# A fused FFN, attention, FFN block on one core: FFN mix read from PSUM, mask merged into the bias, square on ScalarE, 16-bit projections, PSUM banks shared in pairs

## The chip, the core and the metric

The kernel runs on one NeuronCore of a Trainium2 chip. The metric is device time in microseconds (us). The engines are named as the profile names them: PE (TensorE, matmuls), PEld (its weight loads), DVE (VectorE), ACT (ScalarE), POOL (GpSimd) and SP (SyncE, which here issues nearly all DMAs).

## The reference, cut to what matters

Eight sequences of 1024 positions and 256 features go through three residual steps.

```python
x = x + 0.5 * ffn(layernorm(x))
x = x + attn(layernorm(x))
x = x + 0.5 * ffn(layernorm(x))

def ffn(x, W_r, W_k, W_v, mu_r, mu_k):           # x_prev: x shifted by one position, 0 at the start
    xr = mu_r * x + (1 - mu_r) * x_prev
    xk = mu_k * x + (1 - mu_k) * x_prev
    r = sigmoid(xr @ W_r.T)
    return r * (square(relu(xk @ W_k.T)) @ W_v.T)

def attn(x, ...):                                # 16 heads of 16 features
    q, k, v = split(x @ qkv_w.T + qkv_b)
    # 40 offsets: 0..32, 48, 64, 96, 128, 192, 256, 384
    lg[i] = (q . shift(k, o_i)) / 4 * (1 + q @ scale_embed[i]) + pos_bias[i]   # -1e30 where pos < o_i
    out = sum_i softmax(lg)[i] * shift(v, o_i)
    return ((out * if_gain) * sigmoid(x @ gate_w.T + gate_b)) @ out_w.T + out_b
```

## The kernel before, in words

The 8192 rows are cut into 32 chunks of 256 positions and 64 tiles of 128. Five generators hold the work: `stage_f1` (first FFN, by chunk), `stage_p` (the four projections, by chunk), `stage_qk` (scores of queries with local and far keys, by half a sequence), `stage_att` (the rest of the attention, by tile) and `stage_f2` (second FFN, by chunk). A list of steps at the end of the kernel interleaves them, with the stages lagging each other by fixed amounts. Each step gets a priority, and the Tile layer then orders the instructions of each engine by a simulated timeline; each engine executes its own order strictly, waiting on semaphores for the others. So the order on every engine is fixed when the kernel is built.

A chunk of an FFN (`ffn`) takes its PSUM tiles from one bank per lane: tag "ps" plus the lane's letter, "a" for the first FFN and "b" for the second, "p" for the projections. In that bank follow each other the transposed normalized input `tr` (L162), the product with `wk`, that with `wr` and that with `wv` (all recorded at L134, the helper `mm`). Between them stand the copy of `tr` to SBUF with a column for the previous position (`xt`, L186, and the small POOL instructions L183, L185, L189), the difference and the two mixes on DVE (L193, L196), relu and tanh on ACT (L201, L206), the square on POOL (L207), the gating on DVE (L212) and the residual add on POOL (L213).

The projections split the input into `xh` + `xl` and the weights into `wa_hi` + `wa_lo` and add three products for each, in float32r. Each group of q and k goes to DRAM as a 16-bit pair `hl` (L263 on ACT, L264 on DVE). `scores` (in `stage_qk`) multiplies 32-query blocks against keys on 32-column tiles of PE; its results are copied by ACT at L308 (`sl` and `sf`) and written to DRAM in a skewed layout, from where each attention tile reads its logits `lg`.

In `stage_att` `gp` (L134) holds 1 + q.scale_embed before the 1 is added, and DVE multiplies it in at L405 and L410. POOL adds the bias (L419) and, in the first three tiles of a sequence, the mask (L421). After max, subtraction and exp (L423, L424, L425) the probabilities of the 33 near offsets go to DRAM and come back skewed as `pd`, the longest round trip of the tile. The far offsets are multiplied on POOL (L445, `prod`) and added on DVE (L457). PE transposes `pd` in two halves (L464), ACT copies each to `ptt` (L470), and 32 small matmuls of a 32-column tile, 16 after each half, give `pv`. DVE normalizes (L481 to L485), PE transposes `acc` (L490), DVE gates it (L491), and every second tile PE applies the output weights `wot` and DVE adds the result to x (L505).

PSUM has eight banks, used as: one for each of lanes a, b and p, one for scores (`psq`), one for `gp`, one for `pv`, one for the transposes of `pd` (`pst`), and one for the transpose of `acc` and the output product (`psy`).

Of the kernel before, what the change touches and what calls it, by code (L numbers as in the profile page):

```python
# [8 lines left out]
F32 = mybir.dt.float32  # L9
F32R = mybir.dt.float32r  # L10
F16 = mybir.dt.float16
I32 = mybir.dt.int32
AF = mybir.ActivationFunctionType
ALU = mybir.AluOpType
# [25 lines left out]
F2A = 28  # L40
TRACE = (0, 3.6, -4.4, -8.1, -10.6)
# [8 lines left out]
def macaron(ctx: ExitStack, tc: tile.TileContext, x, wffn, watt, wo, cols, rows, pbias, se, mask, out):  # L50
# [14 lines left out]
    bias = const.tile([128, NO * 16], F32, name="bias")  # L65
    msk = const.tile([128, 3, NO], F32, name="msk")
    wa_hi = const.tile([128, 4, 2, 256], F32R, name="wa_hi")
    wa_lo = const.tile([128, 4, 2, 256], F32R, name="wa_lo")
    seb = const.tile([128, 2, NO], F16, name="seb")
    half = const.tile([128, 4], F32, name="half")  # L70
# [18 lines left out]
    def load_ffn():  # L89
        nc.sync.dma_start(w_f, wffn.rearrange("w (c p) d -> p w c d", p=128))  # L90
        nc.vector.tensor_scalar(w_f[:, 2], w_f[:, 2], 0.25, None, ALU.mult)

    def load_att():
        with tc.tile_pool(name="setup", bufs=1) as sp:
            wst = sp.tile([128, 4, 2, 256], F32, name="wst")
            nc.sync.dma_start(wst, watt.rearrange("w (c p) d -> p w c d", p=128))
            nc.vector.tensor_scalar(wst[:, 0], wst[:, 0], 0.25, None, ALU.mult)
            nc.vector.tensor_copy(wa_hi, wst)
            nc.vector.tensor_tensor(wa_lo, wst, wa_hi.bitcast(F32), ALU.subtract)
            nc.vector.tensor_scalar(b_q, b_q, 0.25, None, ALU.mult)  # L100
            nc.vector.tensor_scalar(b_g, b_g, 0.5, None, ALU.mult)
            nc.sync.dma_start(row, rows.unsqueeze(0).to_broadcast([128, 2, 256]))
            for t in [t.bitcast(F32) for t in kb] + vw:
                nc.gpsimd.memset(t, 0.0)
# [8 lines left out]
            nc.sync.dma_start(bias, pbias.to_broadcast([128, NO * 16]))  # L113
            nc.sync.dma_start(msk, mask.rearrange("t p u -> p t u"))
            nc.sync.dma_start(wot, wo.rearrange("(c p) d -> p c d", p=128))
            for c in range(2):
                nc.vector.tensor_scalar(wot[:, c], wot[:, c], gain[:, c : c + 1], 0.5, ALU.mult, ALU.mult)
# [15 lines left out]
    def mm(o, l, r, start, stop):  # L133
        nc.tensor.matmul(o, l, r, start=start, stop=stop)  # L134
# [30 lines left out]
    def ffn(take, done, lane, singles):  # L165
# [3 lines left out]
        for c in range(NCH):  # L169
# [23 lines left out]
            nc.vector.tensor_tensor(xr, xt[:, :, 1:257], prev, ALU.subtract)  # L193
            for o, mu in ((xk, mu_k), (xr, mu_r)):
                for h in range(2):
                    nc.vector.scalar_tensor_tensor(o[:, h], xr[:, h], mu[:, h : h + 1], prev[:, h], ALU.mult, ALU.add)  # L196
# [10 lines left out]
            nc.gpsimd.tensor_tensor(xk, xk, xk, ALU.mult)  # L207
# [25 lines left out]
    def stage_p():  # L233
        for c in range(NCH):
# [10 lines left out]
            nc.vector.tensor_tensor(xl, tr, xh.bitcast(F32), ALU.subtract)  # L245
# [26 lines left out]
            for g in range(2):  # L272
                nc.scalar.activation(gt[:, g], p[:, g], AF.Tanh, bias=b_g[:, g : g + 1], scale=0.5)
# [23 lines left out]
    def stage_qk():  # L297
        def scores(o, g, q4, q, k, keys):

            p = ps.tile([128, 512], F32, name="p", tag="psq")  # L300
# [7 lines left out]
            nc.scalar.copy(o[:, :, :, g], p.rearrange("n (q h j) -> n j h q", q=4, h=2))  # L308
# [60 lines left out]
    def stage_att():  # L369
        for tt in range(B * NT):  # L370
# [27 lines left out]
            for h2 in range(2):  # L398
                gp = ps.tile([128, 64, 8], F32, name="gp")
                for g in range(2):  # L400
# [5 lines left out]
                    lg[:, 0:NL, e], gp[:, 0:NL], 1.0, lg[:, 0:NL, e], ALU.add, ALU.mult  # L406
                )
                for k0, k1 in FARG:
# [4 lines left out]
                        1.0,  # L413
# [172 lines left out]
```

## Time and profile before

| what | value |
|---|---|
| median of 3 runs | 1262.62 us (1255.21 to 1265.52) |
| the profiled execution | 1256.76 us, its span 1254.0 us |
| mean granted PE clock | 0.956 |
| busy PE, PEld | 1089.2, 885.7 us |
| busy DVE, POOL, ACT | 942.6, 766.5, 538.0 us |
| DMA | 282.88 MB, mean 226 GB/s |

The busy time of an engine is the time covered by its instructions. A matmul's interval reaches from its start to the modelled end of its pipeline, and the intervals of successive matmuls overlap, so the distance between their starts is what one of them costs. PEld, the weight loads, runs beside the matmuls. "Idle before, releaser" in a profile row is the time that the engine stood before the instruction, and who ended it. A helper's matmuls all have line L134, so they are told apart by the names of their tiles.

### The profile page before, as it was taken

How to read it: one execution, taken by the hardware profiler on the slowest of the kernel's cores; microseconds unless marked ns; L12 is line 12 of the kernel's file. 1: busy time of each engine (PE TensorE's matmuls, PEld its weight loads, DVE VectorE, ACT ScalarE, POOL GpSimd, SP SyncE). 2: the span in 40 equal slices, each digit the busy share in tenths (PEclk: the TensorE clock that was granted, in tenths of full speed). 3: DMA queues.
4: the chain of work that ended last, by engine and by line, in shares of the span. 5: the costliest groups of instructions: out<-in, count | busy, mean ns of one | idle time of the engine just before them, and what ended most of it. 6: DMA issues, size and time to landing. Idle time of an engine off the chain costs nothing.

```text
span 1254.0 us, 34712 instructions
## 1 busy us (share of the span) xinstructions
PE 1089.2 (87%) x13568; PEld 885.7 (71%) x13568; DVE 942.6 (75%) x2266; ACT 538.0 (43%) x1025; POOL 766.5 (61%) x1101
## 2 busy tenths in 40 slices
PE   2887989899799898989899989899988998888785
PEld 2676768677687677777777778786777787665664
DVE  7546768987587888879678866978858887877772
ACT  2444445344453444536345454544534444524231
POOL 7436619675575656659457564867656755657672
PEclk9999999899999999899999999999989999998988
DMA  8187888786878779787788977797787868998630
GB/s 263 32 224 222 241 242 265 229 238 194 251 226 254 230 233 274 221 252 232 193 260 257 254 201 230 228 269 227 233 243 234 269 197 254 284 280 265 202 99 24
DMA packets 256500, 282.88 MB, mean 226 GB/s; under 512 B 23440, under 2 KB 214608, under 8 KB 256336
## 3 DMA queue, kind: packets, MB, share of 16 engines
q1 hardware_dynamic: 247120, 263.36, 71.7%
q10 hardware_dynamic: 9216, 17.31, 3.8%
q8 instruction: 106, 1.74, 0.6%
q14 instruction: 58, 0.48, 0.1%
HBM read 151.67 MB, written 128.91 MB: 224 GB/s over the span
## 4 chain that ended last, share of the span: by engine, by line
PE 42%; DMA 25%; DVE 14%; SPq 6%; POOL 5%; issue 5%; ACT 4%; POOLq 0%; ACTq 0%; DVEq 0%
PE p L134 29%; DMA pd<-pd 9%; PE tra L464 4%; PE pv L134 3%; PE tra L134 3%; POOL prod L445 2%; DMA lg<-sl 2%; DMA x<-in_x_dram 2%; DMA qk<-hl 2%; DMA kb<-qk 2%; DMA sl<-sl 2%; DVE prod L457 2%; DVE xk L196 1%; PE gp L134 1%; DVE mx L423 1%
## 5 line engine op out<-in xcount | busy, mean ns | idle before, releaser
L134 PEld LDWEIGHTS <-qst 128*32 128x32 f16 (+1 forms) x5120 | 157.2, 120 | 100.1 <-issue 63.5
L134 PE MATMUL p<-kb,qst 128*32 128x128 f16 (+1 forms) x4096 | 185.1, 297 | 12.7 <-ACT sl L308 8.6
L308 ACT COPY sl<-p 128x512 f32<-128x512 f32 x224 | 130.8, 584 | 144.2 <-PE p L134 123.0
L445 POOL TENSOR_TENSOR prod<-v,lg 128x256 f32<-128x256 f32 x248 | 165.5, 687 | 10.2 <-ACT lg L425 6.1
L134 PE MATMUL p<-xk,w_f 128*128 128x256 f32 x512 | 144.9, 421 | 20.0 <-DVE xk L196 11.7
L419 POOL TENSOR_TENSOR lg<-lg,bias 128x640 f32<-128x640 f32 x64 | 113.5, 1774 | 71.8 <-DVE lg L410 66.9
L213 POOL TENSOR_TENSOR x<-x,xr 128x512 f32<-128x512 f32 x64 | 88.4, 1382 | 109.0 <-DVE xr L212 94.9
L457 DVE TENSOR_TENSOR prod<-prod 128x512 f32<-128x512 f32 (+2 forms) x120 | 126.1, 1051 | 32.1 <-POOL prod L445 31.5
L464 PE MATMUL tra<-ident,pd 128*128 128x128 f32 x512 | 97.1, 313 | 58.3 <-DMA pd<-pd 54.9
L160 ACT ACTIVATE xn<-x,nb,y 128x256 f32<-128x256 f32 x192 | 110.8, 602 | 63.0 <-DVE nb L152 55.2
L134 PE MATMUL p<-w_f,xk 128*128 128x256 f32 x512 | 132.9, 400 | 1.7 <-ACT xr L206 1.3
L134 PE MATMUL p<-w_f,xr 128*128 128x256 f32 x512 | 130.4, 396 | 3.6 <-ACT xk L201 2.8
L445 POOL TENSOR_TENSOR prod<-vn,lg 128x256 f32<-128x256 f32 x144 | 96.0, 678 | 54.3 <-ACT lg L425 35.4
L134 PE MATMUL p<-xh,wa_hi 128*128 128x256 f32 x384 | 123.2, 321 | 5.6 <-DVE hl L264 4.4
L134 PEld LDWEIGHTS p<-xk,w_f 128*128 128x128 f32 x512 | 99.3, 208 | 39.8 <-issue 10.5
L470 ACT COPY ptt<-tra 128x512 f32<-128x512 f32 x128 | 74.9, 585 | 116.1 <-PE tra L464 113.0
L464 PEld LDWEIGHTS tra<-ident,pd 128*128 128x128 f32 x512 | 71.0, 197 | 73.9 <-DMA pd<-pd 68.0
L263 ACT ACTIVATE hl<-p,col 128x256 f16<-128x256 f32 x128 | 60.6, 474 | 121.1 <-PE p L134 68.6
L134 PE MATMUL p<-xh,wa_lo 128*128 128x256 f32 x384 | 111.5, 290 | 0.0
L134 PE MATMUL p<-xl,wa_hi 128*128 128x256 f32 x384 | 111.4, 290 | 0.0
L134 PEld LDWEIGHTS p<-w_f,xr 128*128 128x128 f32 x512 | 95.3, 196 | 19.4 <-ACT xk L201 5.8
L134 PEld LDWEIGHTS p<-w_f,xk 128*128 128x128 f32 x512 | 96.0, 198 | 15.9 <-issue 2.8
(82 smaller groups left out, 2394.2 us busy)
## 6 DMA issues: line engine op xcount, KB each, us to landing
qk<-hl SPq DMA_DIRECT2D x256, 128.0 KB, 3.4
sl<-sl SPq DMA_DIRECT2D x256, 128.0 KB, 3.8
pd<-pd SPq DMA_DIRECT2D x64, 512.0 KB, 4.8
sf<-sl SPq DMA_DIRECT2D x184, 128.0 KB, 3.1
vw<-vd SPq DMA_DIRECT2D x128, 136.0 KB, 4.1
v<-vd SPq DMA_DIRECT2D x64, 272.0 KB, 4.3
lg<-sl SPq DMA_DIRECT2D x64, 264.0 KB, 4.1
pd<-lg ACTq DMA_DIRECT2D x64, 264.0 KB, 3.8
```

What stands on the lines that cost most here:

```text
L134: nc.tensor.matmul(o, l, r, start=start, stop=stop)
L160: nc.scalar.activation(xn, x2[:, i], AF.Identity, bias=nb[:, k : k + 1], scale=y[:, k : k + 1])
L196: nc.vector.scalar_tensor_tensor(o[:, h], xr[:, h], mu[:, h : h + 1], prev[:, h], ALU.mult, ALU.add)
L213: nc.gpsimd.tensor_tensor(x2, x2, xr, ALU.add)
L263: nc.scalar.activation(hl[:, 0], p[:, g], AF.Identity, bias=bb[:, g : g + 1])
L308: nc.scalar.copy(o[:, :, :, g], p.rearrange("n (q h j) -> n j h q", q=4, h=2))
L419: nc.gpsimd.tensor_tensor(la, la, bias, ALU.add)
L423: nc.vector.tensor_reduce(mx, lg.rearrange("p u e -> p e u"), AX.X, ALU.max)
L445: nc.gpsimd.tensor_tensor(prod[:, k], shifted[k][1]()[:, :, 0:16], lf[:, k].unsqueeze(2).to_broadcast([128, 16, 16]), ALU.mult,)
L457: nc.vector.tensor_tensor(o, terms[:, 0:m], terms[:, n - m : n], ALU.add)
L464: nc.tensor.transpose(tr[:, pr * 128 : pr * 128 + 128], pd.rearrange("p (m e) -> p m e", e=8)[:, :, 4 * g + pr], ident,)
L470: nc.scalar.copy(ptt.rearrange("p q n -> p (q n)"), tr)
```

## The change

The FFN mix is rewritten. Where `tr` was copied to SBUF and mixed from there, ACT now writes mu * `tr` to `xm`, and DVE adds (1 - mu) * the neighbouring column of `tr` to it, both reading PSUM; the four pieces (two mixes by two halves of the features) alternate between the two engines. The first column of a chunk gets its previous position from `last`, which is now computed on DVE already multiplied by 1 - mu, and added on POOL. The square moves from POOL to ACT.

The projections' weights and inputs are 16-bit pairs instead of float32r pairs; the weights are scaled by 16 (`WS`) beforehand, and the factor is taken out where the results are used (scores, `gp`, gate, output weights).

The mask is added to the bias once, in the setup, into three masked copies of `bias`; a tile adds one of the four.

In PSUM the scores and `gp` share two buffers of one tag, and so do the transposes of `pd`, the transpose of `acc` and the output product. Both halves of `ptt` are copied before the values, and the 32 value matmuls of a tile are issued in one run, the last head first, held behind the first of them.

```diff
-    bias = const.tile([128, NO * 16], F32, name="bias")
-    msk = const.tile([128, 3, NO], F32, name="msk")
-    wa_hi = const.tile([128, 4, 2, 256], F32R, name="wa_hi")
-    wa_lo = const.tile([128, 4, 2, 256], F32R, name="wa_lo")
+    bias = const.tile([128, 4, NO, 16], F32, name="bias")
+    wa_hi = const.tile([128, 4, 2, 256], F16, name="wa_hi")
+    wa_lo = const.tile([128, 4, 2, 256], F16, name="wa_lo")
+    rest = const.tile([128, 4], F32, name="rest")
...
+        nc.vector.tensor_scalar(rest, col[:, 0:4], -1.0, 1.0, ALU.mult, ALU.add)
...
-            nc.vector.tensor_scalar(wst[:, 0], wst[:, 0], 0.25, None, ALU.mult)
-            nc.vector.tensor_copy(wa_hi, wst)
-            nc.vector.tensor_tensor(wa_lo, wst, wa_hi.bitcast(F32), ALU.subtract)
+            nc.vector.tensor_scalar(wst[:, 0], wst[:, 0], 0.25 * WS, None, ALU.mult)
+            nc.vector.tensor_scalar(wst[:, 1:4], wst[:, 1:4], WS, None, ALU.mult)
+            nc.scalar.copy(wa_hi, wst)
+            nc.vector.tensor_tensor(wa_lo, wst, wa_hi, ALU.subtract)
...
+            for t in range(3):
+                nc.gpsimd.tensor_tensor(
+                    bias[:, t], bias[:, 3], msk[:, t].unsqueeze(2).to_broadcast([128, NO, 16]), ALU.add
+                )
...
-            xt = pw.tile([128, 2, 257], F32, name="xt", tag="xt" + s)
-            if c % 4 == 0:
-                nc.gpsimd.memset(xt[:, :, 0:1], 0.0)
-            else:
-                nc.gpsimd.tensor_copy(xt[:, :, 0:1], last)
-            nc.scalar.copy(xt[:, :, 1:257], tr)
+            xm = pw.tile([128, 2, 2, 256], F32, name="xm", tag="xm" + s)
+            for o, mu in ((1, mu_k), (0, mu_r)):
+                for h in range(2):
+                    x_, m = xm[:, o, h], rest[:, 2 * o + h : 2 * o + h + 1]
+                    nc.scalar.activation(x_, tr[:, h], AF.Identity, scale=mu[:, h : h + 1])
+                    nc.vector.scalar_tensor_tensor(x_[:, 1:256], tr[:, h, 0:255], m, x_[:, 1:256], ALU.mult, ALU.add)
+            if c % 4:
+                nc.gpsimd.tensor_tensor(xm[:, :, :, 0:1], xm[:, :, :, 0:1], last, ALU.add)
             if c % 4 < 3:
-                last = pstat.tile([128, 2, 1], F32, name="last", tag="last" + s)
-                nc.gpsimd.tensor_copy(last, xt[:, :, 256:257])
-            xk = pw.tile([128, 2, 256], F32, name="xk", tag="xk" + s)
-            xr = pw.tile([128, 2, 256], F32, name="xr", tag="xr" + s)
-            prev = xt[:, :, 0:256]
-            nc.vector.tensor_tensor(xr, xt[:, :, 1:257], prev, ALU.subtract)
-            for o, mu in ((xk, mu_k), (xr, mu_r)):
-                for h in range(2):
-                    nc.vector.scalar_tensor_tensor(o[:, h], xr[:, h], mu[:, h : h + 1], prev[:, h], ALU.mult, ALU.add)
+                last = pstat.tile([128, 2, 2, 1], F32, name="last", tag="last" + s)
+                nc.vector.tensor_tensor(
+                    last,
+                    tr[:, :, 255:256].unsqueeze(1).to_broadcast([128, 2, 2, 1]),
+                    rest.rearrange("p (o h u) -> p o h u", o=2, u=1),
+                    ALU.mult,
+                )
+            xk, xr = xm[:, 1], xm[:, 0]
...
-            nc.gpsimd.tensor_tensor(xk, xk, xk, ALU.mult)
+            nc.scalar.activation(xk, xk, AF.Square)
...
-            xh = pw.tile([128, 2, 256], F32R, name="xh", tag="xk" + s)
-            xl = pw.tile([128, 2, 256], F32R, name="xl", tag="xr" + s)
+            xh = pw.tile([128, 2, 256], F16, name="xh", tag="xh" + s)
+            xl = pw.tile([128, 2, 256], F16, name="xl", tag="xl" + s)
...
-            p = ps.tile([128, 512], F32, name="p", tag="psq")
+            p = ps.tile([128, 512], F32, name="p", tag="psq", bufs=2)
...
-            nc.scalar.copy(o[:, :, :, g], p.rearrange("n (q h j) -> n j h q", q=4, h=2))
+            nc.scalar.mul(o[:, :, :, g], p.rearrange("n (q h j) -> n j h q", q=4, h=2), WS**-3)
...
-                gp = ps.tile([128, 64, 8], F32, name="gp")
+                gp = ps.tile([128, 64, 8], F32, name="gp", tag="psq", bufs=2)
...
-            nc.gpsimd.tensor_tensor(la, la, bias, ALU.add)
-            if t < 3:
-                nc.gpsimd.tensor_tensor(lg, lg, msk[:, t].unsqueeze(2).to_broadcast([128, NO, 16]), ALU.add)
+            nc.gpsimd.tensor_tensor(la, la, bias[:, min(t, 3)].rearrange("p u e -> p (u e)"), ALU.add)
...
-            pv = ps.tile([128, 2, 8, 17], F32, name="pv")
+            ptt = pw.tile([128, 8, 128], F32, name="ptt")
             for g in range(2):
-                tr = ps.tile([128, 512], F32, name="tra", tag="pst")
+                tr = ps.tile([128, 512], F32, name="tra", tag="pst", bufs=2)
...
-                ptt = pw.tile([128, 4, 128], F32, name="ptt")
-                nc.scalar.copy(ptt.rearrange("p q n -> p (q n)"), tr)
-                for pr in range(4):
-                    for q in range(4):
-                        mm(
-                            pv[32 * q : 32 * q + 32, :, 4 * g + pr],
-                            ptt[:, pr, q:128:4],
-                            vwt[:, q, :, 4 * g + pr],
-                            True,
-                            True,
-                        )
+                nc.scalar.copy(ptt[:, 4 * g : 4 * g + 4].rearrange("p q n -> p (q n)"), tr)
+            pv = ps.tile([128, 2, 8, 17], F32, name="pv")
+            def values(ms):
+                return [
+                    nc.tensor.matmul(
+                        pv[32 * q : 32 * q + 32, :, m], ptt[:, m, q:128:4], vwt[:, q, :, m], start=True, stop=True
+                    )
+                    for m in ms
+                    for q in range(4)
+                ]
+            first = values((7,))[0]
+            with tc.issue_after(first.ins):
+                values((6, 5, 4, 3, 2, 1, 0))
...
-            tr = ps.tile([128, 512], F32, name="tra", tag="psy")
+            tr = ps.tile([128, 512], F32, name="tra", tag="pst", bufs=2)
...
-                p = ps.tile([128, 512], F32, name="tra", tag="psy")
+                p = ps.tile([128, 512], F32, name="tra", tag="pst", bufs=2)
```

Lines of the changed kernel that the prediction names: the mix is at L196 (ACT) and L197 (DVE).

More of the change, by code (lines that the diff above doesn't have):

```diff
@@ L9 @@
 F32 = mybir.dt.float32
-F32R = mybir.dt.float32r
 F16 = mybir.dt.float16
@@ L40 @@
 F2A = 28
+WS = 16.0
 TRACE = (0, 3.6, -4.4, -8.1, -10.6)
@@ L96, in load_att @@
             nc.sync.dma_start(wst, watt.rearrange("w (c p) d -> p w c d", p=128))
-            nc.vector.tensor_scalar(wst[:, 0], wst[:, 0], 0.25, None, ALU.mult)
-            nc.vector.tensor_copy(wa_hi, wst)
-            nc.vector.tensor_tensor(wa_lo, wst, wa_hi.bitcast(F32), ALU.subtract)
-            nc.vector.tensor_scalar(b_q, b_q, 0.25, None, ALU.mult)
+            nc.vector.tensor_scalar(wst[:, 0], wst[:, 0], 0.25 * WS, None, ALU.mult)
+            nc.vector.tensor_scalar(wst[:, 1:4], wst[:, 1:4], WS, None, ALU.mult)
+            nc.scalar.copy(wa_hi, wst)
+            nc.vector.tensor_tensor(wa_lo, wst, wa_hi, ALU.subtract)
+            nc.vector.tensor_scalar(b_q, b_q, 0.25 * WS, None, ALU.mult)
+            nc.vector.tensor_scalar(b_k, b_k, WS, None, ALU.mult)
             nc.vector.tensor_scalar(b_g, b_g, 0.5, None, ALU.mult)
             nc.sync.dma_start(row, rows.unsqueeze(0).to_broadcast([128, 2, 256]))
+            nc.vector.tensor_scalar(bv, bv, WS, None, ALU.mult)
             for t in [t.bitcast(F32) for t in kb] + vw:
@@ L112, in load_att @@
             nc.sync.dma_start(flat(pd_d, NL * 16, (4 * SKEW, 128), (SKEW, 4), (1, SKEW - NL * 16)), zero[:, : 4 * 512])
-            nc.sync.dma_start(bias, pbias.to_broadcast([128, NO * 16]))
+            msk = sp.tile([128, 3, NO], F32, name="msk")
+            nc.sync.dma_start(bias[:, 3].rearrange("p u e -> p (u e)"), pbias.to_broadcast([128, NO * 16]))
             nc.sync.dma_start(msk, mask.rearrange("t p u -> p t u"))
+            for t in range(3):
+                nc.gpsimd.tensor_tensor(
+                    bias[:, t], bias[:, 3], msk[:, t].unsqueeze(2).to_broadcast([128, NO, 16]), ALU.add
+                )
             nc.sync.dma_start(wot, wo.rearrange("(c p) d -> p c d", p=128))
             for c in range(2):
-                nc.vector.tensor_scalar(wot[:, c], wot[:, c], gain[:, c : c + 1], 0.5, ALU.mult, ALU.mult)
+                nc.vector.tensor_scalar(wot[:, c], wot[:, c], gain[:, c : c + 1], 0.5 / WS, ALU.mult, ALU.mult)
             se_f = sp.tile([128, NO], F32, name="se_f")
@@ L241, in stage_p @@
             tr = norm_transposed(x1[c], y, nb, 2 * k, s)
-            xh = pw.tile([128, 2, 256], F32R, name="xh", tag="xk" + s)
-            xl = pw.tile([128, 2, 256], F32R, name="xl", tag="xr" + s)
+            xh = pw.tile([128, 2, 256], F16, name="xh", tag="xh" + s)
+            xl = pw.tile([128, 2, 256], F16, name="xl", tag="xl" + s)
             nc.scalar.copy(xh, tr)
-            nc.vector.tensor_tensor(xl, tr, xh.bitcast(F32), ALU.subtract)
+            nc.vector.tensor_tensor(xl, tr, xh, ALU.subtract)
             def proj(w):
@@ L272, in stage_p @@
             for g in range(2):
-                nc.scalar.activation(gt[:, g], p[:, g], AF.Tanh, bias=b_g[:, g : g + 1], scale=0.5)
+                nc.scalar.activation(gt[:, g], p[:, g], AF.Tanh, bias=b_g[:, g : g + 1], scale=0.5 / WS)
             p = ps.tile([128, 512], F32, name="p", tag="ps" + s)
@@ L405, in stage_att @@
                 nc.vector.scalar_tensor_tensor(
-                    lg[:, 0:NL, e], gp[:, 0:NL], 1.0, lg[:, 0:NL, e], ALU.add, ALU.mult
+                    lg[:, 0:NL, e], gp[:, 0:NL], WS, lg[:, 0:NL, e], ALU.add, ALU.mult
                 )
@@ L412, in stage_att @@
                         gp[:, NL + k0 : NL + k1],
-                        1.0,
+                        WS,
                         ef[:, w0 : w1 + 1 : (w1 - w0) // (k1 - k0 - 1), e],
```

## The prediction

> **What bounds the kernel now.** I read the page first: the busy shares and the chain that ended last.
>
> ```profile
> PE 1089.2 (87%) x13568; PEld 885.7 (71%) x13568; DVE 942.6 (75%) x2266; ACT 538.0 (43%) x1025; POOL 766.5 (61%) x1101
> ...
> PE 42%; DMA 25%; DVE 14%; SPq 6%; POOL 5%; issue 5%; ACT 4%; POOLq 0%; ACTq 0%; DVEq 0%
> ```
>
> TensorE leads both lists, but its busy figure can't be used as a price: matmuls overlap. The timeline of PE in mid-kernel (start, length, instruction, count) shows what one really costs:
>
> ```profile
> 600.23 0.35 PE L134 MATMUL p<-kb,qst 128*32 128x128 f16 x11
> 600.50 0.39 PE L134 MATMUL p<-xh,wa_hi 128*128 128x256 f32 x1
> 600.73 0.27 PE L134 MATMUL p<-xl,wa_hi 128*128 128x256 f32 x1
> 600.84 0.28 PE L134 MATMUL p<-xh,wa_lo 128*128 128x256 f32 x1
> 600.96 1.89 PE L134 MATMUL p<-w_f,xr 128*128 128x256 f32 x8
> ...
> 603.52 0.28 PE L134 MATMUL p<-xl,wa_hi 128*128 128x256 f32 x1
> 603.64 0.29 PE L134 MATMUL p<-xh,wa_lo 128*128 128x256 f32 x1
> 603.86 0.26 PE L134 MATMUL pv<-vw,ptt 128*32 128x34 f32 x2
> ...
> 609.21 0.34 PE L134 MATMUL gp<-seb,qst 128*128 128x40 f16 x5
> ```
>
> A projection matmul lasts 0.28 us, but the next starts 0.12 us later (603.52 to 603.64). An FFN one costs (1.89 - 0.38)/7 = 0.215 us. In starts, PE's work is: FFN and output 1792 x 0.215 = 385 us, projections 1536 x 0.12 = 184, transposes 1024 x 0.11 = 113, scores, gp and values about 205; near 890 of 1254 us. The rest is changes between 128-column and 32-column tiles, restarts, and waits. So PE is the nearest bound, at some 71% by starts and not 87%, and the other 29% is as large a target. PE's waits (total us, times, longest):
>
> ```profile
> PE tra L464 <- DMA pd<-pd: 54.9, 33, 7.2
> PE tr L162 <- ACT xn L160: 26.2, 7, 17.6
> PE p L134 <- DVE xk L196: 11.7, 13, 2.4
> PE gp L134 <- DVE lg L410: 10.1, 9, 2.4
> PE tra L490 <- DVE acc L485: 9.0, 8, 2.3
> PE p L134 <- ACT sl L308: 8.6, 9, 4.4
> ```
>
> Last, the instructions that the FFN mix consists of (minimum/median/maximum ns), and one of the same kind that takes one input from PSUM:
>
> ```profile
> L196 DVE SCALAR_TENSOR_TENSOR xk<-xr,col,xt x128: 441/478/1785, 20.6 to 1239.1; 128x256 f32<-128x256 f32 x128
> L405 DVE SCALAR_TENSOR_TENSOR lg<-gp,lg x128: 363/423/439, 102.7 to 1192.8; 128x264 f32<-128x264 f32 x128
> ```
>
> With two SBUF inputs a 128x256 operation can stretch to 1785 ns (mean 689); with a PSUM input a longer one never passes 439.
>
> **The change part by part.** All against the profiled execution: 1256.8 us, its span 1254.0 and 2.8 around it. The median of the three timed runs, 1262.6, is 5.9 above it.
>
> *16-bit projections.* 1536 matmuls of 256 columns stay 1536, each with a weight load. No row shows a 16-bit matmul of 256 columns. From the row, the ends are 0 (a step of 0.12 us as now) and whatever its f32 weight load costs: that one lasts 197 ns against 105 for the 16-bit 128x128 loads, and gp, with such a load each, steps by (0.34 - 0.20)/4 = 0.035 us, so a 16-bit load would not be the limit. The Trainium skill, "TensorE: Matmul & The Clock Gate", section "Back-to-back issue gap", gives 262 cycles for 256 columns, 109 ns. By the row alone the part is worth 0; by the rule 1536 x 0.011 = 17 us. I take 17, since the row's 0.115 to 0.12 us lies so close to one pass that only a small surplus can go. The tempting sum, the 290 to 321 ns mean of the busy rows less a third of that, gives about 300 us and is wrong by the start times. The casts xh and xl keep their size; the new factors 16 are constants inside existing instructions.
>
> *Values in one run.* In the built order of PE's instructions the 64 tiles' values lie in 169 stretches before and 72 after, and changes between the two tile widths fall from 676 to 549: 64 round trips fewer. One costs: into the wide matmuls 0.12 us (the last score starts near 600.35, the next matmul at 600.50, where scores step by 0.03), 0.11 on the second matmul (600.50 to 600.73 against 0.12), and 0.10 going out (603.64 to 603.86): 0.33 us. 64 x 0.33 = **-21 us**. Both ptt copies now precede the values; that costs the first half 0.585 us of waiting, and PE has other work there.
>
> *PSUM banks in pairs.* Scores had one buffer and gp one; now both rotate through two. The table has 8.6 us for a score behind the copy sl and 10.1 for gp behind L410. Neither vanishes: two gp of a tile fill both buffers, and the next score then stands behind DVE. Transposes of pd and of acc share two likewise (acc 9.0 + 3.3, ptt 2.5 us). Ends: +15 (rotation makes scores wait for gp) and -33 (all gone). I take **-20**.
>
> *FFN mix.* Out per chunk: ACT copy 0.586, DVE subtract 0.81, four DVE operations of 0.68. In: four ACT scalings of 128x256 from PSUM (0.47 by the L263 and L273 rows), four DVE operations with one PSUM input (0.42 by L405), and on 48 chunks `last` on DVE (0.16 by L481) and an add on POOL. DVE: 64 x (0.81 + 4 x 0.26) - 48 x 0.16 = 110 us less, 942 to 832. ACT: 64 x (1.88 - 0.586) = 83 more. Latency is another matter. Here a rule speaks against the change: "PSUM — Partial Sum Buffer", section "PSUM bank collisions raise a hardware error", says that ACT and DVE may not read one bank at once, so they are kept apart. `tr` is one bank. The trace agrees on the nearest pair, hl: ACT L263 waits 46.4 us in 26 cases for DVE L264 on the other half of the same bank. Were the eight free to overlap, they would end after 4 x 0.47 + 0.42 = 2.3 us; by the rule and that row it is 4 x 0.47 + 4 x 0.42 + 0.16 = 3.7, and only then may the wk matmuls take the bank. Before, these started after 0.586 + 0.81 + 2 x 0.68 = 2.8 us: 0.9 later now. I charge no time for that: each of the two lanes has about 34 us for a chunk whose chain is some 10 us. Without that slack it would be 64 x 0.9 = 58 us.
>
> *Square on ACT.* POOL loses 64 x 1.16 = 74 us; ACT gains 64 x 0.66 = 42 (between 0.595 for L201 and 0.74 for the longer L425), and the POOL hop leaves the chain, 0.5 us a chunk. *Mask merged:* POOL loses 24 x 1.32 = 32 us. *Small POOL pieces:* 37 us of memsets and copies go, 48 adds of 0.3 to 0.44 come. The add waits for ACT's fourth scaling, and queued behind it on POOL are bias adds and prod, for which DVE waits; but POOL's waits for ACT and DVE in the old mix go (25 + 33 + 30 + 53 = 141 us idle before L183, L185, L189 and L207). POOL: 766 to about 645. ACT: 538 to about 663.
>
> What is this worth? Chain shares times the relative change: DVE 14% of 1254 x 110/942 = -20; POOL 5% x 121/766 = -10; ACT 4% x 125/538 = +12. Together **-18 us**; from -45 (relief also shortens others' waits) to +15 (ACT's queue).
>
> *Setup.* Three bias adds of about 1.7 us now stand on POOL ahead of the first chunk's inverse roots, and wait for the mask's DMA near 13 us; the roots began at 11.1, so they begin near 18: at most 7, I take **+6**. The cast of wa_hi on ACT ends before its first normalization (16.95). DMAs: the same 1363 on SP, same bytes, no new queue position that matters.
>
> Sum: -17 - 21 - 20 - 18 + 6 = -70: 1186.8, rounded to **1186 us**, range of this case 1150 to 1215.
>
> **The rivals.** (a) *PE's floor.* If shorter DVE and POOL queues remove most PE waits, PE has 890 - 17 of work, about 60 of width changes, 130 of restarts and half-clock stretches, and some 50 at the two ends: about 1115. For it: no other engine would be over 70%. Against: the DMA waits stay. (b) *The pd round trip takes what PE frees.* The longest PE wait is for pd<-pd (54.9), 9% of the chain, with one pd buffer and bytes unchanged. Then the 38 us of PE work and most of the 20 are spent waiting; the 18 and some 10 remain: about 1228. (c) *Nothing:* the gains lie beside the att chain; about 1252. (d) *ACT becomes the queue that PE waits for, slower.* Three of the four scalings in each chunk wait at the head of ACT's queue for DVE: 192 waits where hl has 64 that cost 46.4 us, thus 139 us of standing, with the sl, ptt, relu and xn evacuations queued behind. If half reaches PE (+70) and the -38 of banks and queues is lost, 1186 + 70 + 38 = 1294. It decides the sign from about 70 us passed on to PE. Against it: ACT idles 716 us now, and the standing can lie in that.
>
> **How the numbers follow.** Main case 0.50, (a) 0.17, (b) 0.16, (c) 0.07, (d) 0.10. About 1% is what a measurement here can tell from no change. Faster by over 1%: 0.50 + 0.17 + 0.16 = 0.83; within: 0.07; slower: 0.10. The range runs from (a) to the edge of (c), 1110 to 1247, leaving out (d), most of (c) and a little below (a).
>
> **What would show it.** Right: projection matmuls start 0.11 us apart; L197 near 0.42 us and never past 0.5; DVE about 830, POOL 645, ACT 660 us busy; PE's waits on L410 and sl down. Wrong: the projection step still 0.12; ACT idle at L196 behind DVE over 100 us with PE waiting for ACT; pd's wait well over 55 us (rival b); a first chunk that is not later. The forecast fails as a whole if PE's starts don't come closer although DVE and POOL are lighter.

## The result, and the profile after

The changed kernel is slower. Its median is 1321.13 us (1316.43 to 1329.9, four runs) against 1263.06 us for the kernel before, also of four: a ratio of 1.0485 (1.046 by the medians), with a 95% interval of 1.042 to 1.055. The profiled execution took 1329.9 us, the longest of the four, with a span of 1327.9 us.

From the page of the kernel after, the busy shares and the chain that ended last, by engine and by line:

```profile
PE 1078.8 (81%) x13568; PEld 847.0 (64%) x13568; DVE 835.8 (63%) x2253; ACT 645.7 (49%) x1282; POOL 610.5 (46%) x952
...
PE 41%; DMA 25%; DVE 14%; SPq 5%; POOL 5%; ACT 5%; issue 4%; POOLq 0%; ACTq 0%; DVEq 0%
PE p L144 30%; DMA kb<-qk 7%; DMA pd<-pd 5%; POOL prod L455 4%; DMA qk<-hl 3%; PE tra L474 3%; DVE prod L467 3%; DMA pd<-lg 3%; PE pv L485 2%; DMA qst<-qk 2%; PE tr L172 2%; PE tra L144 2%; DVE mx L433 2%; DVE xm L197 1%; PE gp L144 1%
```

Every engine in the first row but ACT has less to do, and ACT has about as much more as was forecast (108 us, 125 said), and yet the span is 74 us longer. The engine shares of the chain are those of before within a point. They don't say where the time went: a list of busy times or of chain shares can be right in each entry and miss the end by 6%.

The timeline of PE after (start, length, instruction, count), in a run of projections; these answer the rows of 603 us before:

```profile
60.06 0.27 PE L144 MATMUL p<-xh,wa_lo 128*128 128x256 f16 x1
60.17 0.27 PE L144 MATMUL p<-xh,wa_hi 128*128 128x256 f16 x1
60.28 0.27 PE L144 MATMUL p<-xl,wa_hi 128*128 128x256 f16 x1
60.39 0.27 PE L144 MATMUL p<-xh,wa_lo 128*128 128x256 f16 x1
```

From start to start it is 0.11 us now: this distance became as short as forecast. The waits of PE after (total us, times, longest):

```profile
PE p L144 <- DMA kb<-qk: 56.4, 19, 6.0
PE tra L505 <- DVE acc L500: 31.2, 17, 6.6
PE tra L474 <- DMA pd<-pd: 30.9, 24, 3.1
PE tr L172 <- ACT xn L170: 25.5, 6, 22.5
...
PE gp L144 <- ACT sl L320: 10.0, 10, 3.3
...
PE p L144 <- DVE lg L422: 6.6, 15, 1.1
...
PE p L144 <- ACT sl L320: 5.0, 7, 2.1
...
PE gp L144 <- DVE lg L422: 2.8, 4, 1.0
```

The wait for `pd` fell from 54.9 to 30.9. Two others stand in its place: that for `acc` went from 9.0 to 31.2, and the scores wait 56.4 us for keys (`kb`), which cost PE 1.6 us before. The waits for the buffers of scores and `gp` did not shrink but changed partners: a score waited 8.6 us for `sl` and a `gp` 10.1 for DVE's `lg`; now `gp` also waits for `sl` (10.0) and scores for `lg` (6.6), 24.4 us in the four rows against 18.7 in two. These are the places where PE stands, not yet the reason.

The reason shows first in one row of the tile `gp`: its count, its minimum, median and maximum length, then the starts of the first and the last. The row of before, and under it that of after:

```profile
L134 PE MATMUL gp<-seb,qst x1024: 196/207/290, 69.0 to 1192.4; 128*128 128x40 f16 x171
```

```profile
L144 PE MATMUL gp<-seb,qst x1024: 196/207/275, 147.9 to 1252.6; 128*128 128x40 f16 x171
```

`gp` opens a tile of attention. In the kernel after, the first tile opens 79 us later, and the last one 60 us later. So I cut the span of each profiled execution at these two starts. The stretch between them tells how fast the tiles follow each other, and the other two how long it takes to begin and to finish (all in us; the clock is the mean granted PE clock):

| kernel | to the first gp | first to last gp | last gp to the end | span | clock |
|---|---|---|---|---|---|
| before | 69.0 | 1123.4 | 61.6 | 1254.0 | 0.956 |
| after | 147.9 | 1104.7 | 75.3 | 1327.9 | 0.917 |
| before, scores and gp share (e15) | 134.5 | 1098.5 | 72.5 | 1305.5 | 0.932 |
| before, new mix alone (e5) | 71.7 | 1182.9 | 69.0 | 1323.6 | 0.926 |
| before, mix grouped (e10) | 69.4 | 1129.0 | 61.3 | 1259.7 | 0.948 |
| after, scores and gp own (e1) | 74.4 | 1139.5 | 64.3 | 1278.2 | 0.929 |
| after, qk recorded later (e13) | 101.4 | 1105.8 | 76.7 | 1283.9 | 0.928 |
| after, two causes undone (e16) | 73.2 | 1107.7 | 68.4 | 1249.3 | 0.934 |

Two kinds of loss stand apart here. Two pairs of rows differ only in whether scores and `gp` share: before and e15, e1 and after. Sharing delays the opening by 65 and 74 us and the stretch after the last `gp` by 11; the middle gives back 25 and 35 of it. The new mix alone (e5) leaves the opening nearly where it was, stretches the middle by 60 and the end by 7. In the kernel after, where both act, the middle is 19 us shorter than before, so the mix's stretch can't be read from its row. The experiments below take the two apart.

### The profile page after: what moved, and what is told of

Its sections match the earlier page's. It is cut to its first block, busy times and chain, and to the rows that moved or that the text cites. A ratio compares the mean times of both kernels' runs of the same rounds, so it can differ in the third digit from the quotient of the medians.

```text
span 1327.9 us, 34781 instructions
## 1 busy us (share of the span) xinstructions
PE 1078.8 (81%) x13568; PEld 847.0 (64%) x13568; DVE 835.8 (63%) x2253; ACT 645.7 (49%) x1282; POOL 610.5 (46%) x952
## 4 chain that ended last, share of the span: by engine, by line
PE 41%; DMA 25%; DVE 14%; SPq 5%; POOL 5%; ACT 5%; issue 4%; POOLq 0%; ACTq 0%; DVEq 0%
PE p L144 30%; DMA kb<-qk 7%; DMA pd<-pd 5%; POOL prod L455 4%; DMA qk<-hl 3%; PE tra L474 3%; DVE prod L467 3%; DMA pd<-lg 3%; PE pv L485 2%; DMA qst<-qk 2%; PE tr L172 2%; PE tra L144 2%; DVE mx L433 2%; DVE xm L197 1%; PE gp L144 1%
## 5 line engine op out<-in xcount | busy, mean ns | idle before, releaser
L144 PE MATMUL p<-w_f,xm 128*128 128x256 f32 x1024 | 262.2, 400 | 4.8 <-ACT xm L213 2.4
L144 PE MATMUL p<-kb,qst 128*32 128x128 f16 (+1 forms) x4096 | 183.2, 300 | 79.7 <-DMA kb<-qk 56.4
L144 PEld LDWEIGHTS p<-w_f,xm 128*128 128x128 f32 x1024 | 193.4, 199 | 39.7 <-ACT xm L213 4.3
L320 ACT ACTIVATE sl<-p 128x512 f32<-128x512 f32 x224 | 131.6, 600 | 144.4 <-PE p L144 114.6
L197 DVE SCALAR_TENSOR_TENSOR xm<-tr,rest,xm 128x255 f32<-128x255 f32 x256 | 120.4, 474 | 80.1 <-ACT xm L196 79.5
L196 ACT ACTIVATE xm<-tr,col 128x256 f32<-128x256 f32 x256 | 119.7, 473 | 88.0 <-DVE xm L197 58.2
L144 PE MATMUL p<-xm,w_f 128*128 128x256 f32 x512 | 135.9, 411 | 18.7 <-DVE mv L153 7.8
L144 PEld LDWEIGHTS p<-xm,w_f 128*128 128x128 f32 x512 | 100.1, 205 | 37.8 <-POOL xm L199 10.5
L144 PE MATMUL p<-xh,wa_hi 128*128 128x256 f16 x384 | 110.3, 287 | 14.3 <-DVE hl L276 12.3
L474 PE MATMUL tra<-ident,pd 128*128 128x128 f32 x512 | 88.1, 306 | 35.8 <-DMA pd<-pd 30.9
L144 PE MATMUL p<-xl,wa_hi 128*128 128x256 f16 x384 | 110.3, 287 | 0.0
L144 PE MATMUL p<-xh,wa_lo 128*128 128x256 f16 x384 | 110.3, 287 | 0.0
```

Source lines behind the costliest of these rows:

```text
L196: nc.scalar.activation(x_, tr[:, h], AF.Identity, scale=mu[:, h : h + 1])
L197: nc.vector.scalar_tensor_tensor(x_[:, 1:256], tr[:, h, 0:255], m, x_[:, 1:256], ALU.mult, ALU.add)
L320: nc.scalar.mul(o[:, :, :, g], p.rearrange("n (q h j) -> n j h q", q=4, h=2), WS**-3)
L474: nc.tensor.transpose(tr[:, pr * 128 : pr * 128 + 128], pd.rearrange("p (m e) -> p m e", e=8)[:, :, 4 * g + pr], ident,)
```

## The experiments

The ratios are to the kernel before, run beside them on the same chip, with 95% intervals. A short diff stands for each edit. Where the same lines are put into the other kernel, that is said in words.

### One part at a time

**e5: the FFN mix alone.** The kernel before gets the new mix (`rest`, `xm`, the eight alternating operations, `last` on DVE and the POOL add) and nothing else.

```diff
-            nc.scalar.copy(xt[:, :, 1:257], tr)
...
-                    nc.vector.scalar_tensor_tensor(o[:, h], xr[:, h], mu[:, h : h + 1], prev[:, h], ALU.mult, ALU.add)
+                    nc.scalar.activation(x_, tr[:, h], AF.Identity, scale=mu[:, h : h + 1])
+                    nc.vector.scalar_tensor_tensor(x_[:, 1:256], tr[:, h, 0:255], m, x_[:, 1:256], ALU.mult, ALU.add)
```

> The kernel before with the new FFN mix alone (ACT scaling and one DVE operation per piece, both from the PSUM bank of tr; last on DVE, the carry added on POOL); square, banks, projections, mask and values as before. Theory M (the mix is the second cause: eight operations on one bank pass the queues of ACT and DVE in turn, and the carry's add waits for ACT at the head of POOL's queue): slower than before by 20 to 60 us, with the FFN chunks and so the projections coming later. Prediction's own terms: 10 to 20 us faster (DVE 110 us lighter). Rival O (any change of the instruction order costs this much, whatever it does): slower by 20 or so, as each of the other three.

Measured: 1323.62 us, 1.0466 (1.0424 to 1.0508). This part alone costs 59 us, as much as the whole change.

**e4 and e15: the shared banks alone.** In the kernel before, e4 shares both pairs and e15 only the scores with `gp`.

```diff
-            p = ps.tile([128, 512], F32, name="p", tag="psq")
+            p = ps.tile([128, 512], F32, name="p", tag="psq", bufs=2)
-                gp = ps.tile([128, 64, 8], F32, name="gp")
+                gp = ps.tile([128, 64, 8], F32, name="gp", tag="psq", bufs=2)
```

> The kernel before with only the banks of the change: scores and gp share two buffers, the transposes of pd and of acc with the output product share two. R and Y: slower than before, 1310 us or more. Rival A: the prediction's minus 20 for this part, 1240 us, or no change.

> The kernel before with scores and gp sharing two buffers alone. e4 with both pairs shared lost 58 us. Theory R: nearly all of it is here, 1300 to 1325. Rival Y: 1275 or less, with the rest from the pair of transposes.

Measured: e4 1319.48 us, 1.0451 (1.0386 to 1.0516); e15 1307.39 us, 1.0362 (1.0302 to 1.0422). So this part too costs nearly the whole change by itself, 45 of the 58 us by the scores and `gp`. Two parts that cost 59 and 58 us alone make 58 together: they don't add.

**e6, e7, e8: the 16-bit projections, the values in one run, the square on ACT, each alone in the kernel before.**

```diff
-    wa_hi = const.tile([128, 4, 2, 256], F32R, name="wa_hi")
+    wa_hi = const.tile([128, 4, 2, 256], F16, name="wa_hi")
...
-                nc.scalar.copy(ptt.rearrange("p q n -> p (q n)"), tr)
+                nc.scalar.copy(ptt[:, 4 * g : 4 * g + 4].rearrange("p q n -> p (q n)"), tr)
...
-            nc.gpsimd.tensor_tensor(xk, xk, xk, ALU.mult)
+            nc.scalar.activation(xk, xk, AF.Square)
```

The first line of each kind stands here for e6, e7 and e8 in turn.

> The kernel before with the 16-bit projections alone. The trace after shows their start distance at 109 ns against 120: 17 us of PE work less. Prediction's term: 1245 us. Theory M: no harm from here, 1240 to 1262. Rival O: 1270 to 1290.

> The kernel before with the values of a tile in one run alone, after both copies of ptt; banks as before. Prediction's term: 20 us less from fewer changes of tile width, 1240 us. Theory M: about 1240 to 1265. Rival O: 1270 to 1290.

> The kernel before with the square on ACT alone: POOL 74 us lighter, ACT 40 us heavier. Prediction: about 5 us faster, 1257. Theory M: 1250 to 1265. Rival O: 1270 to 1290.

Measured: e6 1266.76 us, 1.0015 (0.9982 to 1.0047); e7 1250.98, 0.9884 (0.9834 to 0.9935); e8 1248.45, 0.989 (0.9847 to 0.9933). The values and the square bring about 1.1% each. The 16-bit projections bring nothing. The longest of PE's waits in e6:

```profile
PE tra L468 <- DMA pd<-pd: 81.7, 35, 4.8
```

It was 54.9 us before. PE gets through its matmuls sooner, and its wait for the same transfer is 27 us longer. The merged mask was not run alone: its three added copies of `bias` find room in SBUF only beside the smaller 16-bit weights.

### Which part of the change costs the time

**e1, e2, e3: the changed kernel with banks of its own** for scores and `gp` (e1), for the transposes of `pd` (e2), for all (e3), one buffer each as before.

```diff
-            p = ps.tile([128, 512], F32, name="p", tag="psq", bufs=2)
+            p = ps.tile([128, 512], F32, name="p", tag="psq")
-                gp = ps.tile([128, 64, 8], F32, name="gp", tag="psq", bufs=2)
+                gp = ps.tile([128, 64, 8], F32, name="gp")
...
-            tr = ps.tile([128, 512], F32, name="tra", tag="pst", bufs=2)
+            tr = ps.tile([128, 512], F32, name="tra", tag="psy")
```

> The changed kernel with one part undone: scores and gp have a bank each again (one buffer each). Theory R (the rotation of the shared scores/gp buffers ties a tile's gp to scores some four tiles further on, which wait for kb<-qk): the head loss of about 33 us and most of the new kb<-qk wait (56 us on PE) go, 1250 us or less. Rival A (the alternation of ACT and DVE on one bank in the FFN mix makes PE wait for ACT): stays at 1310 to 1325. Rival Y (the shared pst/psy buffers hold back the transposes of acc): stays above 1300.

> The changed kernel with another part undone: the transposes of pd have one buffer of their own and the transpose of acc with the output product another, as before; scores and gp stay shared. Theory R: little changes, 1300 to 1325. Rival Y: the wait on acc (31 us on PE) goes, 1280 us or less. Rival A: 1310 to 1325.

> The changed kernel with all PSUM banks as before the change, everything else changed. If the banks alone carry the loss (R, Y or both), the other terms of the prediction's sum are left, 17 for the 16-bit projections, about 20 for the values in one run and 18 for the lighter queues, less 6 in the head: about 1210 us. Rival A: above 1300.

Measured: e1 1279.38 us, 1.0144 (1.0107 to 1.018); e2 1325.08, 1.0502 (1.0438 to 1.0567); e3 1289.84, 1.0218 (1.0177 to 1.0259). The scores and `gp` carry the loss of the banks, 42 us. That is not the whole loss: theory R wanted 1250 or less for e1 and about 1210 for e3, and both missed, so a second cause was left. The transposes don't: undoing their sharing changes nothing that can be told in e2, and costs 10 us in e3. What it does is move a wait. In e2 PE waits 5.6 us for `acc` and 81.4 for `pd`, where after it was 31.2 and 30.9. Two waits that trade places, while the time of the kernel stays, are not two gains.

**e12: the changed kernel with the mix and all banks as before**, so that the 16-bit projections, the values, the square and the mask remain.

```diff
-                    nc.scalar.activation(x_, tr[:, h], AF.Identity, scale=mu[:, h : h + 1])
...
+            nc.scalar.copy(xt[:, :, 1:257], tr)
```

> The changed kernel with both suspects undone: FFN mix and PSUM banks as before; 16-bit projections, merged mask, square on ACT and values in one run kept. By the single runs (0, -14, -14 us and nothing measured for the mask) 1235 us; if mix and banks are the whole loss, faster than before by 1 to 3%. If any order of instructions other than the first one costs, 1265 or more.

Measured: 1247.86 us, 0.9874 (0.9788 to 0.996). The other four parts together are a gain of 1.3% (0.4 to 2.1%), less than the single runs add up to (1235 us); all of the loss lies in the mix and in the banks.

### Why the mix costs 59 us

The four FFN steps of a chunk follow each other in one PSUM bank. I matched the built order of PE with the starts in the trace, matmul by matmul, and took for the first FFN's lane the mean times from step to step over its 32 chunks (us; chunk 1, which runs in lane b, is among them):

| kernel | tr to wk | wk to wr | wr to wv | wv to gated | bank held | between chunks | lane ends at |
|---|---|---|---|---|---|---|---|
| before | 9.2 | 6.6 | 7.9 | 5.7 | 29.5 | 2.6 | 1041.6 |
| e5, mix alone | 15.2 | 7.1 | 6.2 | 4.2 | 32.8 | 1.7 | 1118.8 |
| after | 14.1 | 6.5 | 6.2 | 4.7 | 31.5 | 2.6 | 1110.3 |
| e10, mix grouped | 9.0 | 7.5 | 7.8 | 4.7 | 28.9 | 2.2 | 1007.3 |
| e9, no carry | 14.1 | 6.5 | 6.6 | 3.7 | 30.9 | 1.9 | 1062.0 |
| e11, carry on DVE | 14.0 | 7.1 | 6.2 | 3.8 | 31.2 | 2.3 | 1085.1 |

This lane has the least slack: in the kernel before, its bank is held for 29.5 of every 32 us. The second FFN's lane was free 10.9 us between chunks. In e5 the wk matmuls start 6 us later after `tr`, and the lane ends 77 us later, which is 2.4 us for each of 32 chunks. The waits of ACT and of DVE in e5 (here L187 is the scaling, L188 the DVE operation) show the hand-overs:

```profile
ACT xm L187 <- DVE xm L188: 62.5, 69, 3.3
```

```profile
DVE xm L188 <- ACT xm L187: 71.0, 63, 5.7
```

ACT waits here although a scaling uses nothing that the DVE operation before it writes; what the two have in common is the bank of `tr`. Neither instruction takes longer than 0.55 us, yet one of these waits lasts up to 5.7. There are seven such hand-overs in a chunk, one after the other; the POOL add follows the fourth scaling. I matched the eight operations of each chunk in the same way, and took means over the 64 chunks of both FFNs. In e5 they take 9.0 us from the first start to the last end, 3.8 of these their own durations and 5.2 in the seven hand-overs. In 4.8 of the 5.2 us the engine whose turn it was was busy with other instructions: the next operation stood behind them in its queue. Three kernels take this apart.

**e10: the four scalings first, then the four DVE operations.** The same work, one hand-over from ACT to DVE in place of seven.

```diff
-            for o, mu in ((1, mu_k), (0, mu_r)):
-                for h in range(2):
-                    x_, m = xm[:, o, h], rest[:, 2 * o + h : 2 * o + h + 1]
-                    nc.scalar.activation(x_, tr[:, h], AF.Identity, scale=mu[:, h : h + 1])
-                    nc.vector.scalar_tensor_tensor(x_[:, 1:256], tr[:, h, 0:255], m, x_[:, 1:256], ALU.mult, ALU.add)
+            for o, h, mu in pieces:
+                nc.scalar.activation(xm[:, o, h], tr[:, h], AF.Identity, scale=mu[:, h : h + 1])
+            for o, h, mu in pieces:
+                x_, m = xm[:, o, h], rest[:, 2 * o + h : 2 * o + h + 1]
+                nc.vector.scalar_tensor_tensor(x_[:, 1:256], tr[:, h, 0:255], m, x_[:, 1:256], ALU.mult, ALU.add)
```

> As e5, but all four ACT scalings stand before the four DVE operations, so that the bank of tr is handed over once instead of seven times; carry on POOL kept. The durations add up to the same 3.6 us. Theory H: 1270 to 1290, most of the 59 us back. Theory C: stays at 1305 to 1325.

Measured: 1269.27 us, 1.0054 (1.0028 to 1.008). The loss of 59 us is down to about 7, with every instruction kept. The waits of DVE in e10 on the mix:

```profile
DVE xm L189 <- ACT xm L186: 10.5, 9, 3.0
```

71.0 us have become 10.5; ACT doesn't wait for DVE in the mix any more. The eight operations take 4.7 us from the first start to the last end, with the same 3.8 of durations. So in this kernel it isn't the work or its place that costs, but the order of turns. The lane isn't the whole account of the time, though: in e10 it ends 34 us sooner than before, and the kernel is no faster, so something else sets the end there.

**e9 and e11: the carry of the last position.** e9 leaves out `last` and the add that brings the previous chunk's position into the first column (so these columns lack that term); e11 puts the add on DVE.

```diff
-                nc.gpsimd.tensor_tensor(xm[:, :, :, 0:1], xm[:, :, :, 0:1], last, ALU.add)
+                nc.vector.tensor_tensor(xm[:, :, :, 0:1], xm[:, :, :, 0:1], last, ALU.add)
```

The second line is e11's; e9 has neither.

> As e5 (before with the new mix alone, 1324 us), but the first column of each chunk gets no previous position from the chunk before: the POOL add and last on DVE are left out. Theory C (the add on POOL, behind ACT's fourth scaling and POOL's own queue, delays the wk matmuls and is what costs): back to 1255 to 1275. Theory H (the hand-overs between ACT and DVE on the bank of tr cost, each waiting in an in-order queue): stays near 1300 to 1320.

> As e5, but the carry's add runs on DVE, after the fourth DVE operation, not on POOL (48 more small DVE operations of about 0.16 us). Theory C: 1265 to 1285. Theory H: 1305 to 1325.

Measured: e9 1278.43 us, 1.0142 (1.0074 to 1.021); e11 1288.12, 1.0208 (1.0148 to 1.0268). The carry on POOL is worth about 45 us when it goes and 35 when DVE does it. With e10's 54 this is more than the loss, so the two overlap: the alternation without the carry costs 1.4% (e9), the carry without the alternation 0.5% (e10), both together 4.7% (e5). Neither theory alone is right: theory H missed e9 and e11, theory C missed e10. In e9 and e11 the alternation and its 14 us up to wk remain; the bank is held 1.9 and 1.6 us less in each chunk. In how far the one edit also shortens the waits of the other wasn't separated. The waits of POOL in e5 on the add show how long a four-element column (0.2 us) can be held up:

```profile
POOL xm L190 <- issue: 45.5, 9, 7.5
POOL xm L190 <- ACT xm L187: 37.9, 14, 6.7
```

POOL's queue stands at the add for up to 7.5 us in these rows, with POOL's other work behind it, and the wk matmuls, which read that column, can't start before it is done. In the second row the add waits for ACT's scaling; for the first ("issue") the profile shows no releaser, so what those 45.5 us wait for is open.

### Why sharing delays gp

In the built orders of PE I counted the score groups that stand ahead of each tile's `gp` (a tile has 3.5 of them on average). Before, tile 0's `gp` comes after none, and on average 6.4 more than the tile's share stand ahead. In the changed kernel, in e4 and in e15 tile 0's `gp` comes after 16, tile 8's after 44, tile 16's after 72: at every eighth tile 16 ahead, 15.6 on average over all. Two buffers that rotate are handed out in the order in which the program records the tiles, and the list of steps records a step of `qk` 4.4 tiles ahead of the attention; 4.4 x 3.5 = 15.4 groups. With a bank of its own `gp` was free to go ahead of that order. So the cost should follow the recorded lag, and only while the bank is shared.

**e13 and e14: the lag of `qk` 2.4 tiles in place of 4.4,** in the changed kernel (e13), and as a control in e1, where scores and `gp` have their own banks (e14).

```diff
-TRACE = (0, 3.6, -4.4, -8.1, -10.6)
+TRACE = (0, 3.6, -2.4, -8.1, -10.6)
```

> The changed kernel, all banks shared, with one number changed: the scores' stage leads the attention stage by 2.4 steps in the order in which the program is recorded, not 4.4 (priorities as they are). With the shared buffers gp of a tile then follows about 9 score groups before its own instead of 16. Theory R (the rotation of a shared tag follows the recorded order and so delays gp): faster than the change by 15 us or more, 1305 or less. Rival B (two buffers for both are just too few, whatever the order): no better, 1315 to 1350, since the next scores then wait for gp's readers sooner.

> Control for e13: the same number changed where scores and gp have a bank each. Theory R: the recorded order binds nothing there (gp leads by the same 6.7 groups), 1270 to 1290 as e1 (1279).

Measured: e13 1290.71 us, 1.0215 (1.0154 to 1.0276), 30 us less than the changed kernel; e14 1278.49 us, 1.0126 (1.0066 to 1.0186), the same as e1. The row of `gp` in e13:

```profile
L144 PE MATMUL gp<-seb,qst x1024: 196/207/275, 101.4 to 1207.2; 128*128 128x40 f16 x171
```

The first tile opens at 101.4 us in place of 147.9, with 8 groups ahead in place of 16, and the number of buffers is unchanged. So it is the order of the rotation that makes up most of the loss, 30 of the 42 us that banks of their own give back in e1; for the other 12 a shortage of buffers isn't ruled out. The control is a strict one: e14's built order is that of e1 on every engine, so the number that was changed acts through the shared tag alone. The waits for `kb` go with it: 56.4 us after, 42.7 in e13, 15.2 in e1. The row of e15 says the same from the other side, in a kernel with nothing else changed:

```profile
L134 PE MATMUL gp<-seb,qst x1024: 196/207/274, 134.5 to 1233.0; 128*128 128x40 f16 x171
```

### Both causes, and what is left

**e16: the changed kernel with scores and `gp` on their own banks (the edit of e1) and the mix grouped (that of e10).** The transposes stay shared and the carry stays on POOL.

```diff
+            p = ps.tile([128, 512], F32, name="p", tag="psq")
...
+            for o, h, mu in pieces:
+                nc.scalar.activation(xm[:, o, h], tr[:, h], AF.Identity, scale=mu[:, h : h + 1])
```

> The changed kernel with only the two causes mended: scores and gp a bank each, and the mix with its four ACT scalings ahead of its four DVE operations. If these two are the whole loss: as e12 or better, 1230 to 1255. If the parts' losses overlap with something else: 1265 or more.

Measured: 1257.19 us, 0.9958 (0.993 to 0.9987). Two edits, neither of which takes an instruction out, turn 1.0485 into 0.9958: in this combination the loss is gone. Beside the banks of their own (e1, 1279.38), the grouping is worth 22 us, and not the 54 that it was worth in e10. The waits of PE in e16:

```profile
PE gp L144 <- DVE lg L423: 48.7, 23, 5.3
...
PE tra L475 <- DMA pd<-pd: 16.7, 11, 3.2
PE tra L506 <- DVE acc L501: 9.0, 6, 5.2
PE p L144 <- ACT sl L321: 8.3, 12, 2.9
PE p L144 <- DMA kb<-qk: 8.0, 6, 1.7
```

`pd`, `acc` and `kb` are all low now, and `gp` waits 48.7 us for DVE to empty its one buffer: 10.1 before. In the kernel after, with the shared pair, that wait was 2.8 us, but the pair came at a higher price.

**e17: the square and the values together** in the kernel before, the edits of e7 and e8. **e18: the changed kernel with the mix grouped, the carry on DVE and all banks as before,** the edits of e10, e11 and e3.

> The kernel before with the two parts that each gained: square on ACT (1248) and values in one run (1251); mix, banks, mask and projections as before. If their gains add: 1235. If both take the same slack, as e12 (1248, which has these two and the 16-bit projections and the mask) suggests: 1245 to 1250.

> The changed kernel with all banks as before, the mix grouped (four ACT scalings ahead of four DVE operations) and the carry's add on DVE. If POOL's add is still worth something beside the grouping: 1240 or less. If the grouping has removed the whole delay before the wk matmuls: as e16, 1250 to 1260.

Measured: e17 1263.08 us, 0.9968 (0.9929 to 1.0008); e18 1287.91, 1.0167 (1.0102 to 1.0232). Both missed. Gains of 1.2% and 1.1% should have made 2.3% and made 0.3%. And e18, which was to be the best, is 31 us above e16. It differs from e16 in two edits, the carry on DVE and the transposes on their own banks, and the runs don't separate them; its PE waits 62.3 us for `pd` where e16 waits 16.7. e18 bounds the account of the mix. It differs from e12 in the mix alone, and is 40 us slower; and against e3 the grouping and the carry on DVE together gain nothing clear (1.0218 to 1.0167). So grouping mends the mix in e10 and in e16, but not in every surrounding. The lane of the first FFN isn't what is slow in e18: it ends at 1046.5 us, where that of before ends at 1041.6. Why e18 is slow stays open. Each edit also gives all engines a new order of instructions, and that is a likely reason why effects miss their sum by up to 30 us; it was not shown. A single gain of 1% in these kernels need not be a property of the edit.

No version beats the rest clearly: e12 (1247.86), e8 (1248.45) and e7 (1250.98) are the fastest and lie about 1% below the kernel before.

## Why the prediction was wrong, by its own steps

- **FFN mix, where it failed.** The step was "I charge no time for that: each of the two lanes has about 34 us for a chunk whose chain is some 10 us." The 10 us were a sum of durations. From the first transpose to the gated end, a chunk of the first FFN takes 29.5 us in the trace of before. About 15 of these are pauses between the end of one step and the start of the next, and in 13 of the 15 the engine of the next step was busy with other instructions (means over the 31 chunks of lane a). The slack was 2.6 us, not 24. The rule of the Trainium skill, "PSUM — Partial Sum Buffer", section "PSUM bank collisions raise a hardware error", did speak against the change, and I weighed it and set it aside. The runs agree with it: the two engines take turns on `tr` (62.5 us of ACT's waits in e5), and each turn is a place in a queue. The durations on the bank that I worked out, 3.7 us, were too small a price as well: from first start to last end the eight took 9.0 us, and the wk matmuls came 6 us later and not 0.9. The POOL add was seen in the prediction, but given no time on the way to wk; without it e9 is 45 us faster than e5. "Without that slack it would be 64 x 0.9 = 58 us" matches the measured 59 us only by chance: it was 2.4 us on each of 32 chunks.
- **PSUM banks in pairs, -20 us: the wrong sign.** Measured +45 us for the scores and `gp` alone, outside the ends of +15 and -33. I priced the waits for buffers, which only changed partners (18.7 to 24.4 us). The step that failed is that I did not ask in which order the shared buffers are handed out. The built order of the changed kernel had the answer: 16 score groups stand ahead of tile 0's `gp`, where none stood before.
- **16-bit projections, -17 us.** The step is right: 0.11 us, the rule's value and not the row's. The time isn't: 0 (e6), while PE waited 27 us longer for `pd`. This fits rival (b)'s mechanism at the size of one part.
- **Values in one run, -21 us.** Alone 1.2%, about 15 us (e7), near the size; next to the square it does not add (e17). The reason given does not carry it: in e7's built order the changes of tile width fall from 676 to 642, not to 549. These are 17 round trips, at the prediction's 0.33 us about 6 us (an estimate). That the number came out near is in part luck.
- **Lighter queues, -18 us.** The sizes are good: DVE 836 us busy (832 said), ACT 646 (663), POOL 610 (645). The DVE operation with a PSUM input never passed 0.487 us, as said, where the one with two SBUF inputs reached 1.785; its median is 0.477 us, though, and not 0.42. The square alone brought 1.1%. The worth of the rest can't be told apart from the order effects. To multiply chain shares by changes of busy time was unfounded, for the chain shares hardly moved while the span grew by 74 us.
- **Setup, +6 us.** The first chunk's transposes start at 22.5 us, 17.6 before; the first wait of PE for `xn` is 22.5 us long in place of 17.6. Right.
- **Rivals.** (d) had the sign, a size of 1294 and part of the mechanism. But its signs did not show: ACT stands only 58.2 us at L196 behind DVE, not over 100, and the waits for ACT don't lead PE's list. The standing reaches PE through the lane's late wk matmuls, as the table of the lane has it, and under no wait's name. The rival I lacked was the changed order of a shared tag. Its price lay in one number of the built order and one start time.

The sign that I named at the end, whether "PE's starts don't come closer although DVE and POOL are lighter", could not have told the causes apart either. The start of the first `gp` and the time that a bank is held would have.

## What to carry to other kernels

Before you call a chain slack, measure it in the trace from its first instruction to its last and set it against its period: in this pipeline of in-order queues the sum of durations, 10 us, was a third of the real 29.5. Try to let engines that share a bank take few long turns, not many short ones, since every hand-over is a place in another queue; here it was worth 54 us in one kernel, 22 in another, and nothing clear in a third. And when two stages get one rotating tag, compare the built orders first: a buffer more cost more here than it brought, because it tied the urgent stage to the recorded order of the other.

## What of the hardware was not expected

The granted PE clock fell with the loss: 0.956 before, 0.917 after, between these in most of the experiments. A PE that idles more was also granted less. It is not a full account, since e6 was granted 0.928 and was not slower, and e16 was granted 0.934 at a time below that of before. In PE's largest group the lower clock does not show: within one FFN product the starts lie 0.244 us apart on average before, 0.240 after, 0.243 in e5 and 0.246 in e15. So it seems to fall mostly into PE's pauses; whether it adds to the waits elsewhere wasn't separated.

The other surprise was how little the length of an instruction said: each of the eight operations of the mix lasts 0.38 to 0.55 us in e5 and in e10 alike, and yet the one kernel loses 59 us and the other about 7.
